# Half buckets of 64 sources for layer 2's sums, in a four-layer graph network

## The chip, the cores and the metric

The kernel runs on one core of a Trainium2 chip. The metric is the device time of one execution in microseconds. A profile is one such execution, recorded by the hardware profiler. The engines are PE (matrix products), PEld (its weight loads), DVE (vector), ACT (scalar), POOL and SP (the last two mostly start transfers here).

## The reference

There are 6250 nodes with 160 numbers each (64 scalars and 32 vectors of three components) and 100,000 edges, sorted by their target `dst`. Four layers run one after another. Each normalizes the nodes and applies relu, mixes them linearly, forms a message for each edge, sums the messages per node, mixes again and adds to `x`. Layers 0, 1 and 3 take a message from the node `src` and sum it at `dst`; layer 2 does it the other way round, with `edge_index = stack([src, dst])`:

```python
rhat = edge_attr / norm(edge_attr);  sh1 = SQRT3 * rhat
w = relu(edge_feature @ W_fc1) @ W_fc2          # 224 weights an edge, in five parts w0..w4
src, dst = edge_index
xs, xv = s[dst], v[dst]
out0a = w0 * xs
out0b = w3 * einsum('emi,ei->em', xv, sh1) / sqrt(3)
out1a = (w1 * xs)[:, :, None] * sh1[:, None, :]
out1b = w2[:, :, None] * xv
out1c = w4[:, :, None] * cross(xv, sh1[:, None, :]) / sqrt(2)
agg = segment_sum(concat(out0a, out0b, out1a, out1b, out1c), src, num_segments=N) / 32
```

So the sums of layer 2 go by `src`, in whose order the edges do not lie. All data is float32.

## The kernel before

`Fast.prologue` loads the edge lists, prepares constants, runs the node part of layer 0 (50 blocks of 128 nodes, `nodes_in`), and counts the edges of each bucket of sources. It ends with a flag: where the input is not as regular as the fast path needs (a bucket that is too full, for one), `general` runs in place of `Fast.layers`.

`Fast.layers` then runs `edges(0)`, `edges(1)`, `messages2`, `sums2` and `edges(3)`.

`edges(li)` goes over the 784 tiles of 128 edges, four tiles to a group. POOL gathers the source rows of each tile with one indirect transfer (L1278); PE makes the edge weights (L1267, L1301); ACT copies them out; DVE forms the messages (L1331 to L1339) and a one-hot matrix of 64 columns (L1320); PE multiplies both (L1395). Tiles with even and odd numbers belong to two halves of a window's edges and write to the lower and the upper 64 partitions of `pg`. Every 14 tiles a node block follows (`nodes_out`, `nodes_in`), as a generator whose steps are put between later groups.

`positions` is a generator too. `edges(0)` and `edges(1)` advance it by one step in every third group. It computes, on DVE, the row of the buffer `rec2` that each edge's message goes to: for each bucket `b` a compare (`hit`, L1165), a running sum that starts at the bucket's offset (`cum`, L1167), and a predicated copy (L1170). The offsets come from the counts of the prologue (`count_bucket`, L760 to L765): for buckets with odd numbers the compare itself counts, for the others ACT does.

`messages2` forms layer 2's messages in the order of `dst`, in 196 groups of four tiles, and POOL scatters each tile's 128 rows of 390 numbers to `rec2` (L1514). Ahead of that it stores four blocks of zeros behind the last row (L1426), because the sums may read past it.

`sums2` reads `rec2` in order. A bucket has `BN` = 120 sources, there are 53, and each is read as 16 slots of 128 rows from its start on (2 for the last); rows of other buckets find no column in the one-hot matrix. A group is four slots: one load (L1575, eight groups ahead, 780 KB), the local source number (`loc`, L1578), the one-hot matrix (`oh`, L1606), the parts of the message that were left to be multiplied out (`msg`, L1610 and L1612), and for each slot two products into `pg`, over 192 and 288 columns (L1616, L1618). After each bucket ACT copies `pg` out and a node block follows. The start of each bucket is read into a register of SP. PE, DVE, ACT and SP each work in the order in which the scheduler has put their instructions; SP also carries the stores of the node rows (L1033, L1046, L1047).

Of the kernel before, what the change touches and what calls it, by code (L numbers as in the profile page):

```python
# [20 lines left out]
N = 6250  # L21
E = 100000
P = 128
# [43 lines left out]
BN = 120  # L67
BK = (N + BN - 1) // BN
LASTN = N - (BK - 1) * BN
S = 16  # L70
LASTS = 2
EP = TT * P + S * P
# [617 lines left out]
class Fast:  # L690
# [5 lines left out]
    def __init__(self, tc, a, out, shared, dram):  # L696
        self.tc, self.nc, self.a, self.out = tc, tc.nc, a, out
        self.shared = shared

        self.x = [dram.tile([XR, XW], F32, name=f"x{i}") for i in range(4)]  # L700
        self.table = [dram.tile([r, 160], F32, name=f"table{i}") for i, r in enumerate((N0 * P, N + P, N + P, N))]
        self.skip = {li: dram.tile([XR, w], F32, name=f"skip{li}") for li, w in ((2, 192), (3, 160))}
        self.rec2 = dram.tile([EP, RW], F32, name="rec2")
        self.last = dram.tile([XR, 160], F32, name="last")


    def prologue(self):
# [16 lines left out]
        self.start2 = sh.tile([1, BK], I32, name="start2")  # L724
# [5 lines left out]
        self.zeros_b = sh.tile([P, TT], BF16, name="zeros_b")  # L730
# [21 lines left out]
        nc.vector.tensor_scalar(flt, src, 1.0 / BN, 0.5 / BN - 0.5, op0=ALU.mult, op1=ALU.add)  # L752
        nc.vector.tensor_scalar(flt, flt, 12582912.0, None, op0=ALU.add)
        nc.vector.tensor_scalar(self.src_b, flt, 12582912.0, None, op0=ALU.subtract)
        count = pro.tile([P, BK + 1], F32, name="count")

        def count_bucket(b):
            hit = pro.tile([P, TT], BF16, name="hit", bufs=4)
            if b % 2:
                nc.vector.tensor_scalar(hit, self.src_b, float(b), None, op0=ALU.is_equal, op1=ALU.add,  # L760
                                        accum_out=count[:, b : b + 1])
            else:
                nc.vector.tensor_scalar(hit, self.src_b, float(b), None, op0=ALU.is_equal)
                junk = pro.tile([P, TT], BF16, name="junk", bufs=2)
                nc.scalar.activation(junk, hit, AF.Copy, accum_out=count[:, b : b + 1])  # L765

        with tc.tile_pool(name="nodes0", bufs=2) as wk, \
# [3 lines left out]
            for b in range(N0 + 4):  # L771
# [14 lines left out]
                if b < BK + 1:  # L786
# [5 lines left out]
        po = pro_ps.tile([P, 2, BK + 1], F32, name="ps_off")  # L792
        nc.tensor.matmul(po[:, 0, :], lhsT=self.before, rhs=count, start=True, stop=True)
        nc.tensor.matmul(po[:, 1, :], lhsT=self.ones, rhs=count, start=True, stop=True)
        total = pro.tile([P, BK + 1], F32, name="total")
        nc.vector.tensor_copy(total, po[:, 1, :])
        ends = pro.tile([P, BK + 1], F32, name="ends")
        nc.vector.tensor_tensor_scan(ends, total, self.zeros_b[:, : BK + 1], 0.0, op0=ALU.add, op1=ALU.add)
        nc.vector.tensor_sub(ends, ends, total)
        nc.vector.tensor_copy(self.start2, ends[0:1, :BK])  # L800
        nc.vector.scalar_tensor_tensor(self.off, ends, -1.0, po[:, 0, :], op0=ALU.add, op1=ALU.add)
# [47 lines left out]
        bad = pro.tile([1, 2, P], F32, name="bad")  # L849
# [7 lines left out]
        nc.vector.tensor_scalar(bad[:, 1, 64 : 64 + BK - 1], total[0:1, : BK - 1], float(S * P), None, op0=ALU.is_gt)  # L857
        nc.vector.tensor_scalar(bad[:, 1, 64 + BK : 65 + BK], total[0:1, BK - 1 : BK], float(LASTS * P), None,
                                op0=ALU.is_gt)
# [281 lines left out]
    def positions(self, wk):  # L1141
# [10 lines left out]
        nc.scalar.copy(rs[:, :, 0:3], sq)  # L1152
        yield
# [9 lines left out]
        for b in range(BK + 1):  # L1163
            hit = wk.tile([P, TT], BF16, name="hit2", bufs=2)
            nc.vector.tensor_scalar(hit, self.src_b, float(b), None, op0=ALU.is_equal)  # L1165
# [6 lines left out]
        nc.vector.tensor_copy(to, pos)  # L1172
# [239 lines left out]
    def messages2(self):  # L1412
# [10 lines left out]
        tail = wk.tile([P, 4, RW], F32, name="tail", bufs=1)  # L1423
        nc.vector.memset(tail, 0.0)
        for r in range(TT * P, EP, 4 * P):
            nc.sync.dma_start(self.rec2[r : r + 4 * P, :].rearrange("(p r) c -> p r c", r=4), tail)  # L1426
# [121 lines left out]
    def sums2(self):  # L1548

        nc, tc, li = self.nc, self.tc, 2  # L1550
        es = ExitStack()
        ld = es.enter_context(tc.tile_pool(name="ld_s", bufs=12))
# [7 lines left out]

        def slots(b):
            return S if b < BK - 1 else LASTS

        data, xts, starts = {}, {}, {}
        groups = [(b, g) for b in range(BK) for g in range(0, slots(b), G)]

        def load(b, g):

            m, n = min(G, slots(b)), BN if b < BK - 1 else LASTN
            if g == 0:  # L1570
                starts[b] = nc.values_load(
                    self.start2[0:1, b : b + 1], engines=[mybir.EngineType.SP], min_val=0, max_val=E,
                    skip_runtime_bounds_check_because="a count of edges, of which there are E")
            rt = ld.tile([P, G, RW], F32, name="rt")
            nc.sync.dma_start(rt[:, :m, :],  # L1575
                              self.rec2[ds(starts[b] + g * P, m * P), :].rearrange("(p s) c -> p s c", s=m))
            loc = ld.tile([P, G], F32, name="loc")
            nc.vector.tensor_scalar(loc[:, :m], rt[:, :m, 261], float(-BN * b), None, op0=ALU.add)  # L1578
            data[b, g] = rt, loc
            if g == 0:  # L1580
                rows = slice(1 + BN * b, 1 + BN * b + n)
                xt = nk.tile([BN, XW], F32, name="xt", bufs=8)[:n]
                nc.sync.dma_start(xt, self.x[2][rows, :])
                sk = nk.tile([BN, 192], F32, name="sk_out", bufs=8)[:n]
# [3 lines left out]
        def nodes(b, acc):  # L1588
# [3 lines left out]
            yield from self.nodes_in(3, xt, w_in, nk, p_n, BN * b, slice(0, n), None, 3)  # L1592

        live = []
        for i in range(8):
            load(*groups[i])
        for i, (b, g) in enumerate(groups):
            if i + 8 < len(groups):
                load(*groups[i + 8])
            rt, loc = data.pop((b, g))  # L1600
            n = min(G, slots(b))
            rt = rt[:, :n]
            if g == 0:
                pg = p_g.tile([BN, 480], F32, name="pg")
            oh = wk.tile([P, G, BN], F32, name="oh", bufs=3)
            tt(oh[:, :n], self.iota[:, None, :BN].to_broadcast([P, n, BN]),  # L1606
               loc[:, :n, None].to_broadcast([P, n, BN]), ALU.is_equal)
            msg = wk.tile([P, G, 288], F32, name="msg", bufs=3)[:, :n]
            by3 = lambda v, u: v[:, :, None, :].to_broadcast([P, n, 3, u])
            tt(msg[:, :, 0:192].rearrange("p g (c u) -> p g c u", c=3), by3(rt[:, :, 192:256], 64),  # L1610
               rt[:, :, 256:259, None].to_broadcast([P, n, 3, 64]), ALU.mult)
            tt(msg[:, :, 192:288].rearrange("p g (c u) -> p g c u", c=3),  # L1612
               rt[:, :, 294:390].rearrange("p g (c u) -> p g c u", c=3), by3(rt[:, :, 262:294], 32), ALU.mult)
            for k in range(n):
                first, end = g + k == 0, g + k == slots(b) - 1
                nc.tensor.matmul(pg[:, 0:192], lhsT=oh[:, k, :], rhs=rt[:, k, 0:192], start=first, stop=end,  # L1616
                                 skip_group_check=True)
                nc.tensor.matmul(pg[:, 192:480], lhsT=oh[:, k, :], rhs=msg[:, k, :], start=False, stop=end,  # L1618
                                 skip_group_check=True)
            live = [m for m in live if not (next(m, True) or next(m, True))]  # L1620
            if g + G < slots(b):
                continue
            acc = wk.tile([BN, 480], F32, name="acc")
# [34 lines left out]
def _layout(inputs):  # L1658
# [43 lines left out]
    a["src_t"] = by_tile(i["src"], BK * BN).T  # L1702
# [63 lines left out]
```

## Time and profile before

| | us |
|---|---|
| median of 3 runs | 5309.66 (5302.54 to 5310.14) |
| the profiled execution | 5299.63 |
| its span, from first to last instruction | 5297.8 |
| PE busy | 4419.6 (83%), granted clock 0.88 on average |
| DVE busy | 4113.6 (78%) |
| POOL busy | 3199.1 (60%) |
| ACT busy | 2078.7 (39%) |

Where the stages lie: the first gather of layer 0 starts at 172.0 us, the first scatter of `messages2` at 2369.0, the first product of `sums2` at about 3436.6, the first gather of layer 3 at 4255.8.

How to read it: busy time is a share of the whole span, and the stages have different limits, so each is read for itself. The granted clock is the share of its full speed that PE had; it falls where PE pauses. DMA's share is the mean over 16 engines, and its GB/s count what they moved. The waits name who ended an engine's idle time last.

### The profile page before, as it was taken

To read this page: it belongs to the slowest core of one execution; us is meant where nothing else is said; L and a number is where in the kernel's file an instruction comes from. 1 tells how busy PE (TensorE), PEld (TensorE's weight loads), DVE (VectorE), ACT (ScalarE), POOL (GpSimd) and SP (SyncE) were. 2 spreads that over 40 slices of the span, in tenths; PEclk is the share of its full clock that TensorE was granted. 3 is DMA by queue.
4 is the path that set the end of the run, shared out by engine and by line. 5 is a ranking of instruction groups with operands and counts; after the bars stand their busy time and mean duration, and the time that the engine had idled before them with its cause. 6 is when DMAs were issued, how large, how long until landed. Compare 5 with 4: busy or idle time off the path is not lost. (4 is left out here: it accounts for less than half of the span.)

```text
span 5297.8 us, 77181 instructions
## 1 busy us (share of the span) xinstructions
PE 4419.6 (83%) x22084; PEld 2768.0 (52%) x22084; DVE 4113.6 (78%) x11512; ACT 2078.7 (39%) x6858; POOL 3199.1 (60%) x3143
## 2 busy tenths in 40 slices
PE   6899999998999999965555556499999988878886
PEld 4455555554555555533333334388888844444443
DVE  6688889896898988857777777577777668887787
ACT  5444445443444545523333333222222244434332
POOL 0577777774777777747777777600000067777776
PEclk9999999997998989977777777699999978898888
DMA  3333333322333333336565555487777433333322
GB/s 96 114 94 95 95 95 92 94 73 78 98 101 96 100 96 99 87 123 209 199 207 199 204 198 198 172 287 234 237 234 237 157 88 83 87 82 85 84 81 58
DMA packets 373004, 708.21 MB, mean 134 GB/s; under 512 B 71469, under 2 KB 250890, under 8 KB 372442
## 3 DMA queue, kind: packets, MB, share of 16 engines
q0 software_dynamic: 163072, 349.43, 21.7%
q1 hardware_dynamic: 208914, 353.42, 21.3%
q8 instruction: 180, 2.95, 0.2%
q14 instruction: 254, 2.08, 0.1%
q10 hardware_dynamic: 584, 0.33, 0.0%
HBM read 493.90 MB, written 209.08 MB: 133 GB/s over the span
## 5 line engine op out<-in xcount | busy, mean ns | idle before, releaser
L1278 POOL DMA_INDIRECT ge<-table,rt x2352 | 2378.3, 1011 | 1770.4 <-DMA skip<-sk 828.2
L1395 PE MATMUL pg<-msg,oh 128*64 128x384 f32 x4704 | 1041.3, 563 | 145.7 <-DVE msg L1339 106.2
L1514 POOL DMA_INDIRECT rec<-row,edge_to x784 | 820.1, 1046 | 301.6 <-issue 187.6
L1305 ACT ACTIVATE ws<-pw,rt 128x96 f32<-128x96 f32 x2352 | 693.1, 350 | 768.9 <-PE pw L1301 265.1
L1301 PE MATMUL pw<-w_w2y,hh 100*128 100x192 f32 x3136 | 675.7, 352 | 17.2 <-ACT ws L1307 14.7
L1395 PEld LDWEIGHTS pg<-msg,oh 128*64 128x64 f32 x4704 | 304.3, 148 | 685.2 <-issue 251.2
L1301 PEld LDWEIGHTS pw<-w_w2y,hh 100*128 100x128 f32 x3136 | 529.7, 200 | 226.3 <-ACT ws L1307 124.8
L1338 DVE TENSOR_TENSOR msg<-msg,bank 128x768 f32<-128x768 f32 x588 | 554.6, 943 | 0.0
L1618 PE MATMUL pg<-msg,oh 128*120 128x288 f32 x1668 | 540.7, 405 | 0.0
L1482 PE MATMUL pe<-tb,oh 64*128 64x160 f32 x1568 | 276.0, 410 | 241.4 <-ACT row L1491 239.2
L1334 DVE TENSOR_TENSOR msg<-ws,ge 128x512 f32<-128x512 f32 x588 | 401.4, 683 | 67.4 <-DMA ge<-table,rt 66.1
L1616 PE MATMUL pg<-rt,oh 128*120 128x192 f32 x1668 | 409.3, 327 | 34.1 <-DVE oh L1606 34.1
L1270 ACT ACTIVATE hh<-ph 100x1024 f32<-100x1024 f32 (+1 forms) x336 | 269.4, 802 | 417.4 <-PE pw L1294 182.6
L1331 DVE TENSOR_TENSOR pr<-ge,bank 128x384 f32<-128x384 f32 x588 | 319.4, 543 | 133.5 <-DMA ge<-table,rt 131.9
L1482 PEld LDWEIGHTS pe<-tb,oh 64*128 64x128 f32 x1568 | 208.6, 255 | 393.0 <-ACT row L1491 384.7
L1307 ACT COPY ws<-pw 128x192 f32<-128x192 f32 x1176 | 391.1, 333 | 0.0
L1267 PE MATMUL ph<-ft,w_w1r 12*100 12x512 f32 (+1 forms) x784 | 337.0, 657 | 57.5 <-ACT hh L1270 40.9
L1616 PEld LDWEIGHTS pg<-rt,oh 128*120 128x120 f32 x1668 | 297.6, 183 | 122.4 <-issue 35.3
L1507 DVE TENSOR_TENSOR row<-pw,ev 128x512 f32<-128x512 f32 x196 | 135.2, 690 | 285.3 <-ACT row L1493 271.0
L1456 PE MATMUL ph<-ft,w_w1d 128*128 128x512 f32 x224 | 170.4, 856 | 220.4 <-ACT hh L1458 197.0
L1332 DVE TENSOR_REDUCE dot<-pr 128x128 f32<-128x384 f32 x588 | 342.8, 583 | 0.1
L1339 DVE TENSOR_TENSOR msg<-ge,ws 128x384 f32<-128x384 f32 x588 | 323.0, 549 | 0.0
(485 smaller groups left out, 7278.8 us busy)
## 6 DMA issues: line engine op xcount, KB each, us to landing
rt<-rec SPq DMA_DIRECT2D x208, 780.0 KB
ge<-table,rt POOLq DMA_INDIRECT x2352
ft<-in_ft_dram SPq DMA_DIRECT2D x56, 512.0 KB
ft<-in_ft_dram SPq DMA_DIRECT2D x28, 896.0 KB
dt<-in_dst_w_dram SPq DMA_DIRECT2D x112, 224.0 KB
xt<-x SPq DMA_DIRECT2D x168, 82.0 KB
rec<-row,edge_to POOLq DMA_INDIRECT x784
rt<-in_rec_dram SPq DMA_DIRECT2D x84, 112.0 KB
```

The lines of the kernel that those rows point to most:

```text
L1278: nc.gpsimd.indirect_dma_start(out=ge[:, k, :], out_offset=None, in_=self.table[li], in_offset=bass.IndirectOffsetOnAxis(ap=rt[:, G * g + ...
L1301: nc.tensor.matmul(pw[:, i, :192], lhsT=hh[:, k + i, :], rhs=w2, start=True, stop=True)
L1305: nc.scalar.activation(ws[:, k0 + i, 0:96], pw[:, i, 0:96], AF.Copy, scale=rt[:, G * g + k0 + i, 0:1])
L1307: nc.scalar.copy(ws[:, k0 : k0 + m, 96:192], pw[:, :m, 96:192])
L1332: nc.vector.tensor_reduce(dot, pr.rearrange("p g c u -> p g u c"), AX.X, ALU.add)
L1334: tt(msg[:, :, AW - 64 : AW + 64].rearrange("p g (k u) -> p g k u", k=2), ws.rearrange("p g (k u) -> p g k u", k=2)[:, :, :, 0:64], e0[:, ...
L1338: tt(mvec[:, :, :, 0:64], by3(t1, 64), yv[:, :, :, None].to_broadcast([P, n, 3, 64]), ALU.mult)
L1395: nc.tensor.matmul(pg[half], lhsT=oh[:, k, :], rhs=msg[:, k, :AW], start=t % WT < 2, stop=t % WT >= WT - 2)
L1482: nc.tensor.matmul(pe[:, 2 * h + k // 2, :160], lhsT=oh[rows, (t0 + k) % WT // 2, :], rhs=tb[rows], start=True, stop=True)
L1514: d = nc.gpsimd.indirect_dma_start(out=self.rec2, out_offset=bass.IndirectOffsetOnAxis(ap=self.edge_to[:, t0 + k : t0 + k + 1], axis=0), i ...
L1616: nc.tensor.matmul(pg[:, 0:192], lhsT=oh[:, k, :], rhs=rt[:, k, 0:192], start=first, stop=end, skip_group_check=True)
L1618: nc.tensor.matmul(pg[:, 192:480], lhsT=oh[:, k, :], rhs=msg[:, k, :], start=False, stop=end, skip_group_check=True)
```

## The change

Layer 2's messages are now sorted by half buckets of 64 sources, 98 of them in 49 buckets of 128. The passes over the edges still go by whole buckets: `src_v` holds 1 for an edge whose source is in the lower half of its bucket and 4096 for the upper, and the compare multiplies by it, so that one count and one running sum carry both halves, the upper in steps of 4096. The counts are unpacked in the prologue. The running sums are kept as differences from 1024 times the half bucket's number, so that both fit, and `positions` unpacks them once at its end. The flag also tests that no half holds more than 9 x 128 edges and that no half's start is over 500 from 1024 times its number.

In `sums2`, each half has nine slots of 128 rows, in three groups; a group is three slots of both halves, with two loads (585 KB each). The one-hot matrix has 64 columns a slot, and the products of the two halves alternate, into the lower and the upper 64 partitions of `pg`. Reads are kept from going past the end by a minimum on the starts, and the zeros behind `rec2` are gone.

```diff
-BN = 120
-BK = (N + BN - 1) // BN
...
+BK = (N + P - 1) // P
+BH = (N + HN - 1) // HN
+S, SG = 9, 3
+RH = 1024
+DRIFT, BIAS = 500.0, 512.0
+SHIFT = 4096.0
...
+        nc.vector.scalar_tensor_tensor(flt, self.src_b, float(-P), src, op0=ALU.mult, op1=ALU.add)
+        nc.vector.tensor_scalar(flt, flt, float(HN), SHIFT - 1.0, op0=ALU.is_ge, op1=ALU.mult)
+        nc.vector.tensor_scalar(self.src_v, flt, 1.0, None, op0=ALU.add)
...
-            if b % 2:
-                nc.vector.tensor_scalar(hit, self.src_b, float(b), None, op0=ALU.is_equal, op1=ALU.add,
-                                        accum_out=count[:, b : b + 1])
-            else:
-                nc.vector.tensor_scalar(hit, self.src_b, float(b), None, op0=ALU.is_equal)
+            nc.vector.scalar_tensor_tensor(hit, self.src_b, float(b), self.src_v, op0=ALU.is_equal, op1=ALU.mult,
+                                           **(dict(accum_out=count[:, b : b + 1]) if b % 2 else {}))
+            if b % 2 == 0:
...
+        nc.vector.tensor_scalar(to, to, 6, 10, op0=ALU.arith_shift_right, op1=ALU.logical_shift_left)
...
-            nc.vector.tensor_scalar(hit, self.src_b, float(b), None, op0=ALU.is_equal)
+            nc.vector.scalar_tensor_tensor(hit, self.src_b, float(b), self.src_v, op0=ALU.is_equal, op1=ALU.mult)
...
-        nc.vector.tensor_copy(to, pos)
+
+        nc.vector.tensor_scalar(n2, pos, 1.0 / SHIFT, -0.25, op0=ALU.mult, op1=ALU.add)
+        nc.vector.tensor_scalar(n2, n2, 12582912.0, None, op0=ALU.add)
+        yield
+        nc.vector.tensor_scalar(n2, n2, 12582912.0, None, op0=ALU.subtract)
+        nc.vector.scalar_tensor_tensor(pos, n2, -SHIFT, pos, op0=ALU.mult, op1=ALU.add)
+        yield
+        hit = wk.tile([P, TT], BF16, name="hit2", bufs=2)
+        nc.vector.tensor_scalar(hit, self.src_v, 1.0, None, op0=ALU.is_gt)
+        nc.vector.copy_predicated(pos, hit.bitcast(mybir.dt.uint16), n2)
+        nc.vector.scalar_tensor_tensor(to, pos, -BIAS, to, op0=ALU.add, op1=ALU.add)
...
-        tail = wk.tile([P, 4, RW], F32, name="tail", bufs=1)
-        nc.vector.memset(tail, 0.0)
-        for r in range(TT * P, EP, 4 * P):
-            nc.sync.dma_start(self.rec2[r : r + 4 * P, :].rearrange("(p r) c -> p r c", r=4), tail)
...
-        ld = es.enter_context(tc.tile_pool(name="ld_s", bufs=12))
+        ld = es.enter_context(tc.tile_pool(name="ld_s", bufs=11))
...
-            rt = ld.tile([P, G, RW], F32, name="rt")
-            nc.sync.dma_start(rt[:, :m, :],
-                              self.rec2[ds(starts[b] + g * P, m * P), :].rearrange("(p s) c -> p s c", s=m))
...
+            rt = ld.tile([P, 2, SG, RW], F32, name="rt")
+            for h in range(2):
+                nc.sync.dma_start(rt[:, h], self.rec2[ds(starts[b][h] + g * P, SG * P), :].rearrange(
+                    "(p s) c -> p s c", s=SG))
...
-            for k in range(n):
-                first, end = g + k == 0, g + k == slots(b) - 1
-                nc.tensor.matmul(pg[:, 0:192], lhsT=oh[:, k, :], rhs=rt[:, k, 0:192], start=first, stop=end,
-                                 skip_group_check=True)
-                nc.tensor.matmul(pg[:, 192:480], lhsT=oh[:, k, :], rhs=msg[:, k, :], start=False, stop=end,
-                                 skip_group_check=True)
+            for k in range(SG):
+                first, end = g + k == 0, g + k == S - 1
+                for o, m in ((0, 192), (192, 288)):
+                    for h in range(2):
+                        nc.tensor.matmul(pg[HN * h : HN * h + HN, o : o + m], lhsT=oh[:, h, k, :],
+                                         rhs=(msg if o else rt)[:, h * SG + k, 0:m],
+                                         start=first and o == 0, stop=end, skip_group_check=True)
```

## The prediction

> **What bounds the kernel now.** The kernel is a row of stages, so I read the slices of the page first, to see which engine is full in which stage (one digit is a tenth of 132 us):
>
> ```profile
> PE   6899999998999999965555556499999988878886
> DVE  6688889896898988857777777577777668887787
> POOL 0577777774777777747777777600000067777776
> PEclk9999999997998989977777777699999978898888
> DMA  3333333322333333336565555487777433333322
> ```
>
> POOL shows a steady 7 in layers 0 and 1 (slices 2 to 17), in layer 2's messages (18 to 25) and in layer 3 (32 to 39), and 0 between them. That gap is layer 2's sums, and there alone PE is at 9 with its clock at 9. A steady 7 is a full POOL, as the line of the gathers shows:
>
> ```profile
> L1278 POOL DMA_INDIRECT ge<-table,rt x2352: 942/946/2717, 172.0 to 5270.8; - x196
> ...
>   issue: 565.7, 1857
> ```
>
> One gather takes 0.95 us and 0.30 us of issue (565.7/1857) go ahead of the next: 1.25 us, which is 76% busy. 784 gathers make 980 us, about what layers 0, 1 and 3 each last. So these stages go at POOL's pace, messages2 too (784 scatters of 1.05 us and 0.30), and work on DVE or PE is covered there while it keeps up. The stretches by 10 or 100 us say the same, and what DMA can do:
>
> ```profile
> 2400.00:2500.00 100.00, 59.84 (x320) 39.85 (x322) 75.50 (x163) 37.21 (x109) 77.40 (x75) 0.72 0.58 197
> 3440.00:3450.00 10.00, 10.00 (x51) 8.57 (x50) 7.34 (x15) 0.00 (x0) 0.00 (x0) 1.00 1.02 390
> 3600.00:3700.00 100.00, 100.00 (x536) 84.55 (x535) 72.77 (x217) 21.64 (x86) 0.00 (x0) 1.00 0.71 235
> 4600.00:4700.00 100.00, 80.34 (x436) 42.24 (x434) 81.22 (x243) 42.00 (x149) 76.54 (x78) 0.94 0.30 82
> ```
>
> Columns after the length: PE, PEld, DVE, ACT, POOL busy, granted clock, DMA share, GB/s. The sums (third row) are PE's alone: 100% at clock 1.00, DVE at 73%, DMA at 0.71. PE sums from 3436.6 to 4236, 800 us. Its blocks write their table rows 15.34 us apart (3704.52 and 3719.86).
>
> **Part 1, the sums on PE.** Before, a bucket of 120 nodes has 16 slots, each a product of 192 and one of 288 columns. The timeline has them end to end: 3700.07 to 3700.88, 0.81 us a slot, 12.96 us a bucket, so 2.4 us go to the node products. After, a bucket of 128 nodes has nine pairs of slots, one for each half; a pair is as many columns for two slots, in 64 column strips that may run beside each other. Its price lies between 0.81 us (full overlap) and 1.62 (none). Layers 0, 1 and 3 have this form, alternating halves:
>
> ```profile
> 1503.33 1.51 PE L1395 MATMUL pg<-msg,oh 128*64 128x384 f32 x8
> 1504.77 0.43 PE L1301 MATMUL pw<-w_w2y,hh 100*128 100x192 f32 x1
> ```
>
> The slot above streams 480 columns twice in 0.81 us, 0.84 ns a column, so one of these eight records is 0.32 us and eight in a row 2.58. They took 1.44 until the next product began. Halves do overlap: half of 2.58 is 1.29. I take 0.81 a pair: 7.3 us a bucket. The 0.15 us beyond 1.29 is what leaving this form costs; the new order on PE leaves it four times a bucket for node products, 0.6 us. PE needs 7.3 + 2.4 + 0.6 = 10.3 us a bucket at full clock.
>
> A rule that speaks against the change: the Trainium skill, "TensorEngine Tiling (Array Packing)", Key Properties, says that changing the tiling mode drains TensorE. It gives no figure; the 0.15 us bears it out, and without such drains the sum would be 9.7 us.
>
> **DVE in the sums.** The rows of before:
>
> ```profile
> L1610 DVE TENSOR_TENSOR msg<-rt 128x768 f32<-128x768 f32 x207 | 196.6, 950 | 0.4 <-PE pg L1618 0.4
> L1606 DVE TENSOR_TENSOR oh<-iota,loc 128x480 f32<-128x480 f32 x207 | 135.5, 654 | 98.9 <-PE pg L1618 98.2
> L1612 DVE TENSOR_TENSOR msg<-rt 128x384 f32<-128x384 f32 x207 | 113.9, 550 | 0.0
> ```
>
> 550 ns at 384 elements and 950 at 768 give 150 ns and 1.04 ns an element. A group is now six half slots: 1152 elements 1.35 us, 576 elements 0.75, one-hot 384 elements 0.55, loc 0.165: 2.82 us. Three groups are 8.45 us. All of DVE in this stretch is 581 us, of which the four kinds (loc: 34.1) are 480; 101 us over 51 blocks is 2.0 for nodes. Sum 10.4 us, and 0.5 for its in-order waits on PE and ACT in the node part (0.2 to 0.3 each in the timeline): 10.9.
>
> **DMA in the sums.** A bucket loads six times 599,040 B (3.59 MB) and moves 0.43 MB of node rows, 4.02 MB. In the first 30 us, with loads queued, 371 to 390 GB/s went through at share 1.02. At 380 that is 10.6 us. The pieces shrink from 6240 to 4680 B a partition, whose price no row has; at the steady row's 235/0.71 = 331 GB/s it would be 12.1.
>
> By the Trainium skill, "DMA: Bandwidth & Descriptors", Specifications, HBM gives one core about 358 GB/s; an estimate by it is 11.2 us. This trace had more over 30 us, so the row counts.
>
> SP starts 11 transfers a bucket at 0.33 to 0.47 us, 4.5 us, and reads a second start. Its waits for node rows stand ahead of later loads, but eight groups, some 30 us of work, are loaded by then: no cost. ACT keeps its 3.4 us a bucket (172.9 us over 51).
>
> **The period.** So the bound moves from PE alone to three within 0.6 us: PE 10.3, DMA 10.6, DVE 10.9. Nothing lost: 10.9. But a PE that pauses gets a lower clock: layer 3, where PE is 85% busy, has 0.87 on average from 4300 to 5100 us. 10.3/0.87 = 11.9; I take 12.0. With the idle 15% on top it would be 13.9, the upper end; I think that too far, since layer 3 is held by POOL, which is idle here. 49 buckets of 12.0 and 3 us for first loads twice as big (1.2 against 0.8 MB) and the fill: 591 us against 800, a gain of **209** (ends 263 and 116).
>
> **Part 2, the zero tail.** It goes, with four stores on SP's queue at the start of messages2:
>
> ```profile
> 2327.11 5.56 SPq L1426 DMA_DIRECT2D rec<-tail  x3
> 2334.07 0.30 SPq L1033 DMA_DIRECT2D table<-tb  x1
> 2334.64 6.85 SPq L1046 DMA_DIRECT2D skip<-sk  x1
> 2341.73 3.67 SPq L1047 DMA_DIRECT2D x<-xt  x1
> 2345.44 4.00 SPq L1426 DMA_DIRECT2D rec<-tail  x1
> 2349.48 0.43 SPq L1436 DMA_DIRECT2D ft<-in_ft_dram  x1
> ```
>
> Behind them are layer 1's last table write, then the loads of ft and tb; PE waits 22.7 us for ft. Removed: 5.56 + 4.00 on the queue, and the skip write's 6.85 against 0.7 to 0.95 in the blocks before, 5.9. Together **15.5 us** earlier, and all scatters with it, since POOL paces them. Ends: 9.6 (the stores alone) and 22 (in the new order ft and dt also stand ahead of that last table write). Next late is that table write itself.
>
> **Part 3, counting.** 50 buckets, not 54. A one-input compare of 784 bf16 takes 0.35 us; the new one multiplies by a second tensor. Bounds 0.35 and the 0.955 of the counting form of the same width; I take 0.955, as two-input rows of 784 take 0.96. 25 x 0.955 - 27 x 0.35 = +14, odd buckets -2, five wide and about ten narrow operations +4: +16 us on DVE. It is full from 10 to 60 us only and then under half busy until the node blocks end at 160, each paced by PE and ACT at 2.56 us. On the path: **+3**; +16 without that cover.
>
> **Part 4, ranking in layers 0 and 1.** 50 x (0.955 + 1.835 + 1.031) - 54 x (0.352 + 1.835 + 1.031) = +17.5 us, unpacking at the end +5. Below nothing is excluded: the ranks are ready at 2009, long before layer 1 ends. POOL's gathers cover it, at 153.4 to 154.3 us busy in every 200, whatever DVE does (80 to 94%). **+2**; +22 without the cover.
>
> **Sum.** -209 - 15.5 + 3 + 2 = -219.5. The profiled execution took 5299.63 us (span 5297.8): 5080. It lies 10 us under the median of the three runs, 5309.66; I put 5085.
>
> **Rivals.**
> A. All three hide each other well, DVE's 10.9 decides: 263 saved, 5026 or a little less. For it: eight loads ahead. Against it: three nearly equal engines with in-order queues.
> B. PE's clock and pauses add up, or DMA stays near 331 GB/s: 13.0 to 13.9 a bucket, 5129 to 5173. For it: layer 3's clock.
> C, slower: the alternation 192, 192, 288, 288 does not overlap, and a pair costs 1.62. PE needs 441 x 1.62 + 49 x 3.0 = 861 us against 800; with the first loads and the other terms +53.5: 5353. It decides from 1.50 us a pair on. Against it: the eight records above; for it: these are of one width, and twice as long.
> D. The prologue's test sends the input to the general path, and nothing of this happens. Counted in the drawn sources, the fullest half holds 1128 (1152 allowed), the greatest drift is 352 (500): near nothing.
>
> **Numbers.** Forecast (11 to 13 us a bucket, 5030 to 5130) 0.63; A 0.13; B 0.16; C 0.06; D 0.02. The range leaves out C, D, the far ends of A and B: 5025 to 5170. 0.2% (11 us) is about what can be told from no change: faster 0.91, same 0.02, slower 0.07.
>
> **What would show it.** Right: in the sums PE is no longer 100% busy, its clock is under 1.00, DVE is over 85%, DMA moves over 320 GB/s, and their first and last products are under 640 us apart; the first scatter comes about 15 us earlier in its stage; POOL's 76% in layers 0 and 1 stays. Wrong: records of the two halves that start end to end; loads that PE waits for at under 300 GB/s; gathers waiting for DVE; a first gather later than 185 us.

## The result, and the profile after

The changed kernel takes 5254.15 us (median of 4 runs, 5251.99 to 5260.95); the kernel before took 5309.76 beside it. The ratio is 0.990 (0.988 to 0.992). The prediction was 5085 us, from 5025 to 5170: the direction was right, and three quarters of the forecast gain did not come. The profiled execution took 5252.15 us, its span is 5250.3 (5297.8 before).

The stages, from one landmark of the profile to the next, in us:

| stage | before | changed | difference | predicted |
|---|---|---|---|---|
| until the first gather of layer 0 | 172.0 | 178.6 | +6.6 | +3 |
| layer 0, until the first gather of layer 1 | 1098.8 | 1146.1 | +47.3 | +2 for both |
| gathers of layer 1 | 1034.1 | 1048.1 | +14.0 | |
| last gather of layer 1 to first scatter | 64.1 | 56.1 | -8.0 | -15.5 |
| first scatter to first sums product | 1067.7 | 1071.3 | +3.6 | 0 |
| sums, until the first gather of layer 3 | 819.2 | 706.0 | -113.2 | -209 |
| layer 3 | 1042.0 | 1044.1 | +2.1 | 0 |

So of the 172 us between forecast (-219.5) and span (-47.5), 96 lie in the sums, 59 in layers 0 and 1, and 17 in all the rest.

The slices of the changed kernel, one digit for 131 us:

```profile
PE   6799999998999999995565655558888788888886
DVE  6688888888788888785777777757777678878786
POOL 0577777774677777774777777740000077777776
PEclk9999989898899899997776677779999988888887
DMA  3333333332333333335556565568777533333332
```

In the sums (POOL 0) PE fell from 9 to 8 as intended, but nothing else became full: DVE is at 7, DMA at 7 or 8. The stretch of 200 us (columns as in the prediction) says it closer, and the rows of DVE show that this is not for want of a right price:

```profile
3720.00:3920.00 200.00, 164.35 (x1246) 97.08 (x1248) 145.99 (x397) 44.96 (x182) 0.00 (x0) 0.97 0.78 277
```

```profile
L1636 DVE TENSOR_TENSOR msg<-rt 128x1152 f32<-128x1152 f32 x147 | 198.7, 1352 | 0.0
L1638 DVE TENSOR_TENSOR msg<-rt 128x576 f32<-128x576 f32 x147 | 110.4, 751 | 0.0
L1632 DVE TENSOR_TENSOR oh<-iota,loc 128x384 f32<-128x384 f32 x147 | 81.0, 551 | 0.0
```

Each operation costs what the prediction said (1.35, 0.75, 0.55), DVE is 73% busy, PE 82%, 277 GB/s move, and a bucket takes 14.13 us. No engine is full. The timeline of one bucket shows why; read it by the last bracket, which is the idle time before an instruction and who ended it:

```profile
3712.73 0.47 ACT L1085 COPY at<-pt_out 128x384 f32<-128x384 f32 x1
3713.25 0.46 PE L1098 MATMUL po<-w_osr,at 96*128 96x96 f32 x2 [0.79 <-ACT at L1085]
3713.55 0.83 PE L1100 MATMUL po<-w_ovw,at 128*128 128x96 f32 x6
3714.31 0.55 PE L1644 MATMUL pg<-rt,oh 128*64 128x192 f32 x4
3714.42 0.26 DVE L1119 TENSOR_TENSOR os__95153<-po,sk_out 128x96 f32<-128x96 f32 x1 [2.83 <-PE po L1100]
...
3717.47 0.17 DVE L1628 TENSOR_SCALAR loc<-rt 128x6 f32<-128x6 f32 x1
3717.55 1.35 DVE L1636 TENSOR_TENSOR msg<-rt 128x1152 f32<-128x1152 f32 x1
3718.82 0.55 DVE L1632 TENSOR_TENSOR oh<-iota,loc 128x384 f32<-128x384 f32 x1
...
3719.42 0.55 PE L1644 MATMUL pg<-rt,oh 128*64 128x192 f32 x4 [1.37 <-DVE oh L1632]
...
3724.97 0.75 DVE L1638 TENSOR_TENSOR msg<-rt 128x576 f32<-128x576 f32 x1
3726.04 0.33 PE L1078 MATMUL pt_out<-ident,acc 128*128 128x128 f32 x1
...
3727.38 0.46 PE L1098 MATMUL po<-w_osr,at 96*128 96x96 f32 x2 [0.79 <-ACT at L1085]
```

DVE stands still for 2.83 us at the first addition of the node step (L1119), which needs PE's `po`. PE's `po` stands in its queue behind a whole group's products, the last transposition (3726.04) and ACT's copy of it. Then DVE does 3 us of node work, and only behind it the next one-hot matrix; for that PE waits 1.37 us (3719.42), having run out of prepared groups. PE waits for DVE, DVE for PE: 14.13 us is one round through both queues, and neither engine's own work.

The gathers, in the whole run, and the waits of POOL in layer 0 (us in all, times, longest), first before and then as changed:

```profile
L1308 POOL DMA_INDIRECT ge<-table,rt x2352 | 2397.0, 1019 | 1710.1 <-DMA ft<-in_ft_dram 717.6 <-issue 569.7 <-DVE bank L1345 178.1
```

```profile
POOL ge L1278 <- issue: 196.2, 644, 0.3
POOL ge L1278 <- DMA ge<-table,rt: 12.2, 40, 0.3
POOL ge L1278 <- DVE pr L1331: 3.7, 12, 0.3
```

```profile
POOL ge L1308 <- issue: 198.3, 650, 0.5
POOL ge L1308 <- DVE msg L1367: 14.0, 6, 2.7
POOL ge L1308 <- DVE xt L1059: 11.1, 9, 3.8
POOL ge L1308 <- DVE bst L1009: 9.9, 10, 2.2
```

Before, no pause of POOL between two gathers of a layer is longer than 0.32 us, whoever is named as its end: POOL was issuing the next gather and had no free time while the gathers ran. Issue takes what it took, but in the changed kernel 24 pauses of layer 0 are longer, until DVE's products (L1367) or whatever DVE finished last; they take 38.3 us beyond 0.30 us each. Gathers waiting for DVE were a sign of "wrong" in the prediction.

### The profile page after: what moved, and what is told of

It is laid out like the page before. It is cut to its first block, busy times and chain, and to the rows that moved or that the text cites. A ratio compares the mean times of both kernels' runs of the same rounds, so it can differ in the third digit from the quotient of the medians.

```text
span 5250.3 us, 77176 instructions
## 1 busy us (share of the span) xinstructions
PE 4243.3 (81%) x22204; PEld 2453.6 (47%) x22204; DVE 4085.3 (78%) x11194; ACT 2067.3 (39%) x6802; POOL 3218.8 (61%) x3143
## 4 chain that ended last, share of the span: by engine, by line
DVE 16%; PE 16%; DMA 13%; POOL 8%; issue 7%; ACT 3%; SPq 0%; DVEq 0%; ACTq 0%; POOLq 0%
DMA rec<-row,edge_to 6%; DMA ge<-table,rt 6%; POOL rec L1540 4%; PE pg L1644 4%; POOL ge L1308 4%; PE pg L1425 2%; DVE msg L1368 2%; PE pw L1331 1%; DVE msg L1636 1%; DVE msg L1364 1%; PE po L1100 1%; DMA rt<-rec 1%; DVE row L1533 1%; DVE pr L1361 1%; PE ph L1482 1%
## 5 line engine op out<-in xcount | busy, mean ns | idle before, releaser
L1425 PE MATMUL pg<-msg,oh 128*64 128x384 f32 x4704 | 1048.1, 566 | 153.2 <-DVE msg L1369 125.6
L1331 PE MATMUL pw<-w_w2y,hh 100*128 100x192 f32 x3136 | 675.7, 353 | 14.3 <-ACT ws L1337 11.8
L1297 PE MATMUL ph<-ft,w_w1r 12*100 12x512 f32 (+1 forms) x784 | 361.7, 659 | 67.3 <-ACT hh L1300 50.1
L1644 PE MATMUL pg<-rt,oh 128*64 128x192 f32 x1764 | 234.5, 345 | 101.5 <-DVE oh L1632 101.3
L1644 PE MATMUL pg<-msg,oh 128*64 128x288 f32 x1764 | 308.6, 429 | 8.3 <-DVE msg L1638 2.8
L1495 PE MATMUL pw<-w_w2d,hh 64*128 64x224 f32 x1568 | 292.7, 461 | 7.9 <-DVE row L1537 7.9
```

The lines of the kernel that those rows point to most:

```text
L1297: nc.tensor.matmul(ph[:, i], lhsT=w1[r : r + K, :], rhs=ft[r : r + K, 4 * P * (j // 2) :][:, : 4 * P], start=True, stop=True)
L1331: nc.tensor.matmul(pw[:, i, :192], lhsT=hh[:, k + i, :], rhs=w2, start=True, stop=True)
L1425: nc.tensor.matmul(pg[half], lhsT=oh[:, k, :], rhs=msg[:, k, :AW], start=t % WT < 2, stop=t % WT >= WT - 2)
L1644: nc.tensor.matmul(pg[HN * h : HN * h + HN, o : o + m], lhsT=oh[:, h, k, :], rhs=(msg if o else rt)[:, h * SG + k, 0:m], start=first and o ...
```

## The experiments

All are changes of the kernel before or of the changed kernel, compared with the kernel before, which ran beside each on the same chip. For the eight runs of experiments 1 to 6 it took 5304 to 5307 us, with a mean granted clock of 0.88. For the ten of experiment 7 it took 6903 to 7133, with a clock of 0.76; layers 0, 1 and 3 and the messages of layer 2 are longer there, so these runs are told by themselves and none is set against the first eight.

**1. The ranking of before in the changed kernel.**

```
- scalar_tensor_tensor(hit, src_b, b, src_v, is_equal, mult)
+ tensor_scalar(hit, src_b, b, None, is_equal)
...                                   # the offsets too are those of whole buckets
- (the operations that unpack the ranks)
+ tensor_copy(to, pos)
```

> The changed kernel with the ranking of before: the compare is again one operation with a constant (352 ns), one plain rank to a bucket of 128, no unpacking behind it. The counting before layer 0 and the sums stay as changed. The messages are then ordered by whole buckets only, so each half's sums take rows that belong to both halves: that part of the result is not the reference's, and the work of the sums is the same. Theory (the packed compare costs layers 0 and 1 all the time that they lost, 47 + 14 = 61 us): the gathers of layer 0 last 1099 us again, those of layer 1 1034, the time is 5195 us (5185 to 5210). Rival 1 (only the compares' own extra DVE time, 51 times 0.61 us = 31 us, comes back): 5223 us. Rival 2 (the prediction: the gathers hide the compare, and the lost time is from something else, such as the changed order of instructions): 5252 us.

Measured: 5195.0 us, ratio 0.980 (0.978 to 0.981). Layer 0 lasts 1096.0 us, the gathers of layer 1 1035.0; the sums stay at 703.8. The whole loss of these layers came with the ranking. The first gather stays late, at 178.0, so those 6 us belong to the counting, which was left in.

**2. The packed compare alone, in the kernel before.**

```
- tensor_scalar(hit, src_b, b, None, is_equal)
+ scalar_tensor_tensor(hit, src_b, b, ones_b, is_equal, mult)
```

> The kernel of before with one thing changed: the ranking's compare is the three-operand form with a multiplication by a tile of ones (as priced: 955 ns for 352). Nothing else of the change is in it. Theory (this compare alone slows layers 0 and 1): layer 0 longer by some 47 us, layer 1 by some 14, 5371 us in all (5355 to 5380). Rival 1 (its own DVE time and no more, 54 times 0.61 us = 33 us): 5343 us. Rival 2 (the prediction: hidden behind the gathers): 5312 us.

Measured: 5373.0 us, ratio 1.013 (1.011 to 1.015): layer 0 +39.6, gathers of layer 1 +20.0. One instruction 50 or so times, 0.35 to 0.96 us long, costs 66 us in the time and 60 in these two stretches, where its own duration adds 33. Both runs together exclude the order of the other instructions as the cause, and the prediction's cover.

The stretch of layer 0 by windows, in the kernel before, with the ranking of before in the changed kernel, and in the changed kernel (one fence for each):

```profile
180.00:1270.00 1090.00, 1028.60 (x5138) 599.86 (x5137) 954.07 (x2673) 525.31 (x1647) 798.13 (x778) 0.93 0.33 91
```

```profile
180.00:1270.00 1090.00, 1026.42 (x5132) 597.61 (x5131) 952.68 (x2669) 526.71 (x1648) 800.12 (x783) 0.93 0.35 93
```

```profile
180.00:1320.00 1140.00, 1060.14 (x5136) 614.82 (x5137) 972.26 (x2670) 528.83 (x1649) 807.19 (x783) 0.91 0.34 89
```

PE is 94% busy before; POOL is at 73%, but has only its issue between the gathers. The same count of products takes PE 32 us longer and the clock falls from 0.93 to 0.91. Counted over layer 0 exactly, from before to changed, PE's idle time rises from 65.8 to 81.3 us, and the stretches at half clock take 100.7 us of PE's speed instead of 77.6; with the packed compare alone the two are 77.1 and 98.0, with the ranking of before 65.3 and 74.0.

What the time went to shows in POOL's own instructions, by their starts and ends (us):

| | gathers' own time, layer 0 | layer 1 | POOL's pauses beyond 0.30 us each, layer 0 | layer 1 | last gather of layer 0 to first of layer 1 |
|---|---|---|---|---|---|
| before | 804.3 | 796.5 | 0 | 0 | 55.9 |
| ranking of before, in the changed kernel | 801.8 | 797.3 | 0 | 0 | 55.7 |
| packed compare alone | 809.3 | 808.9 | 25.4 | 7.6 | 65.2 |
| changed | 808.3 | 810.4 | 38.3 | 0 | 61.0 |

The gathers of layer 1 by windows (POOL busy, clock, DMA share, GB/s), before and as changed:

```profile
1270.76:2305.80 1035.04, 796.51 (x784) 0.92 0.35 96
```

```profile
1324.70:2373.80 1049.10, 810.36 (x784) 0.92 0.36 95
```

So the 61 us of the changed kernel are 18 us of slower gathers, 38 us of pauses and 5 us behind layer 0's last gather. In its layers 0 and 1 a gather that runs beside a packed compare takes 1.25 us on average (64 of them), any other 1.02; with the packed compare alone it is 1.21 (74) and 1.02, and before, beside the one-input compare, 1.06 (49) and 1.02. What holds such a gather up is not in the profile.

**3. The sums in another queue order.** DVE's compare and products (`front`) are written one group ahead, and an ordering edge, without a semaphore, puts node steps on DVE behind them.

```
+ front(i + 1)                       # loc, oh, msg of the next group
  ... products of group i on PE ...
+ with tc.issue_after(last[-1].ins): # last DVE product of front(i + 1)
      live = [m for m in live if not (next(m, True) or next(m, True))]
```

> The changed kernel; in the sums DVE's compare and products of a group are written one group ahead of its TensorE products, and DVE takes up a bucket's node steps only behind them. The same work in another order on the in-order queues. Theory (a bucket's 14.1 us are a cycle through in-order queues: DVE waits 2.8 us a bucket at the first addition of the node step for po, while PE's po stands behind a group's products and a copy by ACT): that wait goes, the period falls to about 12 us (11.4 to 12.6; PE's 11.4 busy and DVE's 10.6 are next), 49 buckets times 2.1 us = 103 us less than 5254: 5151 us (5125 to 5185). Rival 1 (the loads bound the stage): the period stays at 14 us, 5254 us. Rival 2 (PE's granted clock falls to 0.87 once PE is busy nearly without a pause): 11.4/0.87 = 13.1 us, 5204 us.

Measured: 5114.1 us, ratio 0.964 (0.962 to 0.966): 140 us less than as changed, more than expected. The sums take 570.4 us for 706.0. Two views, the windows and DVE's timeline:

```profile
3720.00:3920.00 200.00, 189.95 (x1600) 125.03 (x1602) 187.63 (x514) 57.33 (x231) 0.00 (x0) 1.00 0.99 359
```

```profile
3703.32 0.75 DVE L1638 TENSOR_TENSOR msg<-rt 128x576 f32<-128x576 f32 x1
3704.40 0.26 DVE L1119 TENSOR_TENSOR os__95436<-po,sk_out 128x96 f32<-128x96 f32 x1 [0.33 <-PE po L1100]
```

The wait of 2.83 us is down to 0.33, PE is 95% busy, DVE 94%, the clock is 1.00, and the first additions of two buckets lie 11.25 to 11.28 us apart. The same work in the same kernel, in another order, is 2.9 us a bucket shorter.

The changed kernel itself holds a control: in its queues DVE has three prepared groups in front of the first addition for the first four buckets and two for all later ones but the last, and PE's `po` stands behind two groups of the next bucket for the second to the seventh bucket, behind one from the eighth on. Its first four periods are 11.2 to 11.4 us; from the eighth on they are 13.9 to 15.8, mostly 14.1. With the ordering edge the order stays at three and two.

**4. The zero tail put back into the changed kernel.**

```
+ nc.vector.memset(tail, 0.0)
+ for r in range(TT * P, (TT + 16) * P, 4 * P):
+     nc.sync.dma_start(rec2[r : r + 4 * P, :], tail)
```

> The changed kernel with the removed zero tail put back at its old place: the memset of a tile and four DMAs into 2048 rows behind the messages' own rows. The prediction's price is 15.5 us (5270 us). By the trace, which shows 8.0 us less between the last gather of layer 1 and the first scatter, 5262 us. If these 8 us came from the ranking's last steps and not from the tail: 5254 us.

Measured: 5262.6 us (0.9925, 0.990 to 0.995). The stretch between last gather and first scatter is 64.4 us with the tail and 56.1 without: 8.3 us are the tail's, and the ranking's last steps have no share in it.

**5. The length of DVE's stretches.** Three runs: the packed ranking in three steps (compare, running sum, copy), one after every second group, the plain ranking of before in one step after every sixth, and the first of these with the reordered sums.

```
  scalar_tensor_tensor(hit, ...)
+ yield
  tensor_tensor_scan(cum, hit, ...)
- if li < 2 and i % 3 == 0:
+ if li < 2 and i % 2 == 0:
```

and in the kernel before

```
  tensor_tensor_scan(cum, hit, ...)
- yield
  copy_predicated(pos, hit, cum)
- if li < 2 and i % 3 == 0:
+ if li < 2 and i % 6 == 0:
```

> The changed kernel; the ranking's compare (0.96 us) stands in a step of its own, so that DVE is held 1.84 us at most by the rank's scan instead of 2.80 us by compare and scan together. A bucket's three steps come after every second group, its two steps came after every third: 31 buckets fall into layer 0 either way, and DVE's work is the same. Theory (a long stretch on DVE opens a pause in PE, the granted clock is halved for some windows behind it, and that is why 18.5 us of DVE work cost layer 0 47 us, at a clock of 0.911 for 0.928): the clock of layer 0 returns to about 0.93, layer 0 lasts 1118 us for 1146, the time is 5226 us (5215 to 5235). Rival (only the amount of work on DVE counts): layer 0 stays at 1146 us, 5254 us.

> The kernel of before; a bucket's compare, scan and conditional copy (0.37, 1.84 and 1.03 us) stand in one step after every sixth group instead of two steps after every third. The same work on DVE, in longer stretches. Theory (long stretches on DVE lower PE's granted clock): layer 0's clock falls from 0.93 to about 0.91, layer 0 is 20 us longer, the time 5330 us (5320 to 5345). Rival (only the amount of work counts): 5309 us (5304 to 5314).

> Both: the sums in the new order and the ranking in thirds. By the theory of the stretches 5114 - 28 = 5086 us; by its rival 5114 us, as with the sums alone.

Measured: in thirds 5222.5 us, 0.984 (0.983 to 0.986), for 0.990 as changed. In one step 5326.9, 1.004 (1.003 to 1.006). Both times are as the theory of stretches had them: the same work costs 0.6% less in shorter and 0.4% more in longer pieces. The path was not quite as told. In thirds layer 0's clock is 0.918, not 0.93, and in its profile, which is of the slowest of five executions, layer 0 takes 1135 us, not 1118. In one step the clock of layer 0 falls by 0.007 only, 9 us of half-speed loss, while layer 0 is 27.6 us longer. POOL's pauses in layer 0 carry more: in thirds 9.3 us for 38.3 as changed, in one step 33.5 for none before. So a longer stretch on DVE makes POOL wait longer, and the clock carries only part of the cost. The spacing of the steps changes with their length, and the two are not separated. With the reordered sums, thirds give 5092.9 us, 0.961 (0.958 to 0.964): the fastest time of the study, with an interval that overlaps that of the reordered sums alone.

**6. A third of the loads left out, with the reordered sums.**

```
+ if g + SG == S and kept:
+     rt = kept[0]          # rows of the first bucket's last group, no load
```

> The kernel with the reordered sums, and a third of its loads left out: the last group of each bucket takes the rows that were loaded for the first bucket's last group, so the sums are not the reference's. PE, DVE and ACT do the same work. There PE is busy 95%, DVE 94% and the DMA engines 99% of an 11.2 us period. If the loads set that period, it falls to what PE and DVE need, 10.6 us: 49 times 0.6 = 29 us less, 5085 us. If PE's or DVE's order sets it: 5114 us.

Measured: 5110.0 us, 0.964 (0.962 to 0.965); the sums take 571.9 us, as with all loads.

```profile
3720.00:3920.00 200.00, 189.61 (x1646) 142.44 (x1642) 184.81 (x529) 57.12 (x234) 0.00 (x0) 1.00 0.79 266
```

DMA's share falls from 0.99 to 0.79 and the stage keeps its time, but the run changed more than the loads: the scheduler put a bucket's first addition on DVE up to 14 groups behind the bucket's last one, where it was three. The first thirteen periods are 10.0 to 16.4 us and those from the 21st on 10.95 on average for 11.26; first to last product take 534.7 us for 551.1, and the work behind the last product 37.2 for 19.3. So this run alone does not settle what the loads cost. The waits of experiment 3 do: there no engine waits for a load after 3560 us, 50 us into the node steps, although DMA's share is 0.99. The loads were not its limit; PE at 95% and DVE at 94% set the period together, and which of the two is not separated.

**7. The runs at a clock of 0.76.** First the sums with `front(i + 1)` written ahead as in experiment 3, but without the ordering edge:

```
+ front(i + 1)
  live = [m for m in live if not (next(m, True) or next(m, True))]
```

> The changed kernel with only the first half of the reordering: compare and products of a group are written one group ahead of its TensorE products, without the rule that DVE takes up node steps behind them. Queue orders are made by the program's scheduler; in the built kernel DVE's first node addition still stands behind the same number of groups, and PE's po too. Theory (the queue order is what counts): 5254 us as changed (5245 to 5262). Rival (writing ahead is enough): 5114 us.

Measured: ratio 0.979 (0.975 to 0.984). The sums alone compare, since their clock is 0.97 there too: 703.9 us, as changed (706.0). Writing ahead in the source changed the queue order for the first seven buckets only; from the eighth on it is that of the changed kernel, and so is the period.

Then two kernels on the ranking's open question: with the reordered sums, the scan in two halves, and in the kernel before, a small needless operation.

```
+ yield                                   # behind the compare
+ for o in (0, TT // 2):
+     tensor_tensor_scan(cum[:, o : o + TT // 2], ...); yield
- if li < 2 and i % 3 == 0:
+ if li < 2 and i % 9 % 2 == 0:
```

```
+ if li < 2 and i % 2 == 0:
+     nc.vector.tensor_scalar(extra, oh[:, 0, :16], 1.0, None, op0=ALU.add)
```

> The kernel with the reordered sums; the ranking's scan is cut into two halves of 392 columns, and compare, half scan, half scan and conditional copy are four steps after five of every nine groups. DVE's work is that of thirds (one more instruction a bucket), its longest stretch is 1.03 us instead of 1.84 (thirds) and 2.80 (as changed). Layers 0 and 1 take 26 and 25 buckets instead of 31 and 20. Theory (a stretch costs in proportion to its length: one step instead of two cost 20 us for 1 us more): 17 us less than with thirds, 5076 us (5060 to 5090). Rival (below 2 us a stretch is hidden, only DVE's work is left): as with thirds, 5093 us.

> The kernel of the ranking in quarters once more, because the chip of its first run granted PE a clock of 0.77 to the kernel of before, where all runs until then had 0.87 to 0.88, which stretches layers 0, 1 and 3. Expected as there: by the theory of the stretches 5076 us (5060 to 5090), by its rival 5093 us.

> The kernel of before with a needless DVE operation (128 x 16, some 0.18 us) behind the one-hot compare of every second group in layers 0 and 1: 98 times 0.18 us = 18 us more DVE work in each of them, in pieces and evenly spread, nearly what the packed compare adds to layer 0 in one long stretch per bucket (31 times 0.61 = 19 us). Theory (the length of a stretch is what makes a us on DVE cost more than a us): layer 0 longer by its 18 us or less, layer 1 by 12 to 18, 5305 + 30 to 36 = 5338 us. Rival 1 (the work itself costs 2.5 times its duration in layer 0): layer 0 +45, layer 1 +15 to 20, 5367 us. Rival 2 (small pieces fall into pauses): 5305 to 5315 us.

Measured: quarters 0.971 (0.967 to 0.974) and 0.969 (0.966 to 0.972), small pieces 1.000 (0.998 to 1.003). Then these four beside each other, for what was still open:

> Small pieces again (18 us more DVE work in each of layers 0 and 1, spread over every second group; nothing else differs from the kernel of before). With a clock near 0.88 on the kernel of before: if the length of a stretch is what costs, at most the work itself, +30 to 36 us (ratio 1.006); if the amount costs 2.5 times its duration, +62 us (1.012); if small pieces fall into pauses, 0 to +5 (1.000). With a clock near 0.77: 1.000, as in the first run.

> The reordered sums with the ranking as changed, on the same chip as the next two, for comparison: ratio 0.964 at a clock near 0.88.

> Reordered sums, ranking in thirds (longest stretch 1.84 us for 2.80): ratio 0.961 at a clock near 0.88, 20 us less than with the ranking as changed.

> Reordered sums, ranking in quarters (longest stretch 1.03 us): by the theory of the stretches 17 us less than thirds (0.957); by its rival the same as thirds (0.961).

Measured: pieces 0.999 (0.997 to 1.002), reordered sums 0.958 (0.955 to 0.961), thirds 0.975 (0.972 to 0.979), quarters 0.967 (0.963 to 0.971). And once more:

> Small pieces once more. At a clock near 0.88: if the length of a stretch is what costs, at most the work itself, +30 to 36 us (1.006); if the amount costs 2.5 times its duration, +62 us (1.012); if small pieces fall into pauses, 0 to +5 us (1.000). At a clock near 0.76: 1.000, as in two runs.

> Reordered sums with the ranking in quarters once more. At a clock near 0.88: 5076 us by the theory of the stretches (0.957), 5093 us by its rival (0.961). At a clock near 0.76: 0.968, as in three runs.

Measured: pieces 1.001 (0.999 to 1.004), quarters 0.970 (0.966 to 0.974).

Two readings. The reordered sums keep their gain at both clocks: 571.2 us there too. And splitting the ranking, which gained at 0.88, loses here: thirds are 1.7% behind the same kernel with the ranking as changed. Against giving much weight to that stands layer 3, whose code is the same in all four: in their profiles it takes 1610.5 to 1673.6 us, so a stage that nothing was changed in moves by as much as most of what is compared. The theory of stretches fits the runs at a clock of 0.88; quarters and small pieces were measured at 0.76 only, so it is not a rule.

The windows of layer 0 in the run with small pieces show where the longer time lies:

```profile
180.00:1740.00 1560.00, 1235.95 (x5131) 702.90 (x5131) 961.28 (x2769) 526.05 (x1647) 777.31 (x778) 0.78 0.24 64
```

DVE and POOL are busy about as long as before (961 us with the pieces and 777 us, for 954 and 798), a gather takes 1.00 us for 1.03, and yet layer 0 lasts 1571 us for 1099. PE is busy 209 us longer, at the lower clock, and it is idle 328 us instead of 66. Two of its waits, with small pieces and before (us in all, times, longest):

```profile
PE ph L1269 <- ACT hh L1272: 93.8, 32, 8.1
PE pw L1303 <- ACT ws L1309: 58.7, 21, 26.0
```

```profile
PE ph L1267 <- ACT hh L1270: 16.0, 18, 1.2
PE pw L1301 <- ACT ws L1307: 7.8, 32, 0.7
```

ACT itself waits there, 128.8 us ahead of `hh` alone, for signals whose sender the profile does not show. So the clock is less than half of the difference, and what opens the long pauses stays unknown. POOL's gathers pause 479 us beyond their issue in this layer, which leaves room for small pieces on DVE.

## Why the prediction was wrong, point by point

**Part 1, the sums.** The prices nearly held: DVE's rows are within 3 ns, its work is 10.6 us a bucket for 10.4 and PE's 10.7 for 10.3 (94% and 95% of 11.26 in experiment 3), loads move at 359 GB/s there, between the 331 and 380 considered, and the halves do overlap. In the changed kernel's timeline a pair of 192 and 288 columns for both halves recurs every 0.81 us:

```profile
3715.74 0.50 PE L1644 MATMUL pg<-rt,oh 128*64 128x192 f32 x4
3716.07 0.65 PE L1644 MATMUL pg<-msg,oh 128*64 128x288 f32 x4
3716.55 0.49 PE L1644 MATMUL pg<-rt,oh 128*64 128x192 f32 x4
```

So rival C is out. The step that failed is "0.5 for its in-order waits on PE and ACT in the node part (0.2 to 0.3 each in the timeline): 10.9", and with it "So the bound moves from PE alone to three within 0.6 us". The waits were read from a kernel in which PE was 100% busy and DVE had 27% to spare; there they cost nothing, so they said nothing of what they cost when both are nearly full. They are 2.83 us a bucket on DVE, and PE's pauses beside them. The period here is a round through the queues, not the largest sum of one engine's work. With the order mended the period is 11.26 us, near the 10.9 of DVE alone: the three-engine sum is near what the work allows, and rival A was near what the sums could do (-249 us), not what they did.

The allowance for the clock, 12.0 for 10.9, was put on the smaller loss. The clock in the sums is 0.97: ten stretches of 3.41 us at half clock, and the periods of 15.5 to 15.8 us start a few us ahead of them. In the reordered sums, where PE hardly pauses, there is none. So the pauses did lower the clock; but they were the loss themselves, 14.13 for 11.26, and the clock took only a further 1.3 to 1.7 us in every third to fifth bucket. (10.3/0.87 is 11.8, not 11.9; nothing hangs on it.)

The Trainium skill, "TensorE: Matmul & The Clock Gate", Part 1, has the gate in two states, half and full, judged by windows of 3.4 us. The traces agree: every clock record here is 0.5 or 1.0, and all but one in each trace last multiples of 3.41 us. The page's table names at least one idle window as the condition for half speed; in the changed sums pauses of 1.4 us and less came with it. The same page's section "A second HAM failure mode: psum-queue depth-cycling" says that frequent short idle times between products make the gate swing, without giving a length.

Rival B had the sums' outcome almost by number (13.0 to 13.9 a bucket), partly by luck. PE's pauses came, though from the queues; the low clock did not (0.97 for 0.87), nor did slow loads: in experiment 3 all of them go through in an 11.26 us period.

**Part 2, the tail.** -8.3 us for -15.5. The stores' own 9.6 us were the lower end, and that is all there was. The term of 5.9 us for the skip write behind them failed: skip writes still take 2.97 and 5.61 us on SP's queue in the changed kernel, where loads stand between them, so taking the stores away did not give that time back.

**Part 3, counting.** +6.6 us for +3, within the end of 16; experiment 1 shows that it stays when the ranking goes.

**Part 4, the ranking.** The step that failed is "POOL's gathers cover it, at 153.4 to 154.3 us busy in every 200, whatever DVE does", and with it the +2 us. The price of the compare was right (963 ns for 955) and so was the sum of work (by its own terms +17.3, not +17.5). The reading ahead of it, "A steady 7 is a full POOL", holds for the kernel before: no pause over 0.32 us between gathers. Only its figure was low: it took the median of a gather, 0.95 us, where the mean is 1.03 in layer 0, so 784 gathers take 1043 us and not 980, and 56 us more lie behind the last one. But a full POOL covers nothing that touches its own queue. Gathers took longer, 18 us in all, some 15 of them in the 64 that ran beside the compare (0.23 us each); others came late, 38 us; and POOL had no free time in which to make that up. Experiments 1 and 2 show the cost in both directions (63 and 60 us, of which the work is 31 to 33). PE's longer pauses and lower clock in layer 0 came with it; what share they have in DVE being late stays open, and so does whether evenly spread work would cost less than itself at 0.88. At 0.76 spread work costs nothing that can be measured, in layers where POOL pauses for other reasons.

**What would have shown it beforehand.** The built kernel's queue orders were there to be read: how many groups DVE has prepared when it comes to the first addition, and how many PE must finish first.

**What to do.** The reordered sums are the version to keep: 0.964 (0.962 to 0.966) of the kernel before at a clock of 0.88, 0.958 (0.955 to 0.961) at 0.76.

## What to carry to other kernels

When a change makes several engines nearly full, do not take the largest of their sums: walk once round the in-order queues, with the instruction that waits, what it waits for, and what stands ahead of that, and see whether the round is longer than any one engine. An engine at a steady 75% can be full: add the issue to its operations, by their mean and not their median, and look at the longest pause between two of them (0.32 us here). Such an engine covers other engines' work only while that work neither slows its operations nor keeps them waiting, since it cannot make up a pause; before counting on cover, ask what its next operation waits for, and how late that may come.

## What the runs showed of the hardware that was not expected

The DMA engines can show a share of 0.99 at 359 GB/s while no engine waits for a load (the sums of experiment 3, after 3560 us). A one-input compare of 784 bf16 values takes 0.35 us on DVE and a two-input one 0.96 us, and the difference, some 50 times, cost 60 us of a kernel whose DVE was 78% busy; gathers that POOL ran beside the two-input form took 1.25 us for 1.02. The granted clock of the same kernel was 0.88 in some runs and 0.76 in others, both on one chip; layers 0, 1 and 3 took 1.3 to 1.6 times as long at 0.76, and the sums took the same, also where their PE pauses (82% busy: 703.9 us for 706.0).
